# A graph layer with sorted edges on one core: spare edges of two sets at once, and single VectorE operations where there were several

## The chip, the cores and the metric

The kernel runs on one core of a Trainium2 chip. Its time is the device time of one execution in microseconds (us), and the median of several executions is what counts. Five engines work side by side, each on its own list of instructions in a fixed order: TensorE multiplies matrices, VectorE and ScalarE work element by element, GpSimd here issues the gathers (indirect DMAs), and SyncE issues the other DMAs. They wait for each other through semaphores. An engine that waits does nothing else, since it doesn't look past the instruction that waits.

## The reference

There are 12,500 nodes with 128 features each, and 400,000 edges sorted by their destination. Each edge has a type, 0 or 1.

```python
Xs = X[src]
m_data = Xs @ W_data.T + b_data
m_ctrl = Xs @ W_control.T + b_control
msg = jnp.where((edge_types == 0)[:, None], m_data, m_ctrl)
agg = jax.ops.segment_sum(msg, dst, num_segments=X.shape[0])
out = jax.nn.relu(agg + (X @ W_self.T + b_self))
x = _layernorm(x + out, axis=-1)
```

Since the sum is linear, the kernel first sums the rows `X[src]` by destination and type, and multiplies each sum with the weights afterwards. A row is kept as three bf16 parts whose sum is the f32 value.

## The kernel before

**Tiling.** 128 edges are a chunk. 125 chunks are a group, and there are 25 groups. A group alternates between windows of 5 chunks and windows of 20 chunks. For the short windows the rows of `x` are gathered from DRAM by indirect DMAs (`fetch`, L720, 865 gathers of 128 rows). For the long ones, called **sets** here, nothing is gathered: `x` lies whole in SBUF (`x3`), and rows are picked out of it by matmuls with one-hot matrices. There are 113 sets of 2,560 edges. The main loop (L1010) runs over them.

**What is done for a set.** The source of an edge is node `src & 127` of block `src >> 7`. Each of 98 blocks (100 cells with two spare ones) gets 32 places per set, and every edge has to find a place in its block's row.

1. `block_matrix` (L528) compares each edge's block with all cells: `O`, 128 x 2000. `fours` (L545) adds it up over chunks, and `same_lane` (L533) counts earlier edges of the same lane with the same block.
2. `before` (L550): TensorE multiplies the sums with a triangular matrix into the PSUM tile `rk`. `ranks` (L562) on VectorE turns this into the rank of each edge in its block: `ahead`, `prod`, three folding additions into `half`, a reduction `found` (L578) and `rank`.
3. `rank_matrix` (L602): `rm` compares the rank with 0 to 31, and two multiplications (L607) give `rv`: where the rank fits, the edge's node in one half and its code in the other (the code is its destination's offset and its type).
4. `put` (L614): 20 matmuls of `O` with `rv` write node and code of every place into `rk`. `spread` (L624) copies them out on ScalarE (`cell`), stores the nodes to DRAM (`there`) and loads them back to all 128 partitions (`pick`, 128 x 3200, 800 KB). SyncE issues both.
5. `pick_matrix` (L657): VectorE compares `pick` in place with the lane's number, in two halves. The result is the one-hot matrix.
6. `picked` (L774), one set later: 24 + 1 quads of matmuls `got` (L790) pick the rows out of `x3`, ScalarE copies them to SBUF (`emsg`, L802), VectorE makes the one-hot matrices of destinations (`esel`, L481, three for each set), and the matmuls `sums` (L676) and counts (L814) add the rows up in PSUM. `accumulate` (L707) adds that to `acc` in SBUF.

**Spare edges.** An edge whose rank is 32 or more has no place. `over` (L582) finds them: `key` keeps the packed source and code of such edges, `top` takes a lane's largest 8, and from these come their number (`over_n`) and three numbers of each (`bits`: block, node and code), copied to bf16 on ScalarE. `spare_slots` (L489) gives them up to 64 places of a further cell: the matmul `over_before` (L496, L497) counts those of lower lanes, `over_matrix` (L501) makes the one-hot matrix `om`, `turn` (L505, L507) multiplies it with `bits`, and `keep` (L512) leaves the code with the set's others and the row number in `idx` (L518). `spare_rows` (L767) gathers these rows while the set is being picked.

**Order.** In turn w of the main loop, set w is picked and added up while the places of set w + 2 are made, and the spare edges of set w + 1 get theirs. Each piece of work has a position between 0 and 1 in the turn, `merged` (L141) sorts the pieces by it, and the framework, when it builds the program, moves instructions within each engine's list again by its own estimate of when their inputs are there. So `pick`, `esel` and the work for other sets stand between the steps of `ranks`. In VectorE's list as built, the steps from `ahead` to the second `rv` stand in one run with these between them. On TensorE `put` stands within the last quads of the set that is being picked.

Beside this, each group needs once: `prep_e` (L457) and `prep_p` (L435), which prepare the codes of its edges (`erel`, L463, the destination minus the window's first one, in five operations), the pass of an overlap to the next accumulator (L700), and `finish` (L870), which multiplies the sums with the weights, normalizes and stores.

## Time and profile before

| | us |
|---|---|
| median of 3 runs (1954.3 to 1966.5) | 1956.54 |
| the profiled execution | 1946.23 |
| its span, first to last instruction | 1944.4 |
| TensorE matmuls busy | 1753.1 (90%) |
| VectorE busy | 1717.1 (88%) |
| GpSimd busy | 1362.6 (70%) |
| ScalarE busy | 1303.0 (67%) |

The granted clock of TensorE was 0.986 on average. No engine is busy all the time, and the two busiest are close to each other, so it has to be read from the waits which one holds up the other. A mean duration in the groups runs from an instruction's start to its end; the next one on VectorE starts some 0.07 to 0.09 us before that end where it needn't wait for the result (`esel` takes 0.878 us, and the next instruction starts 0.802 us after it). For sums along VectorE's list the distance from start to start is used, which the timeline shows.

The span has three stages: until about 127 us `x` is split and stored and the first sets are prepared; until about 1890 us the main loop runs; the rest ends the last group.

### The profile page before, as it was taken

The page shows a single profiled execution, that of the slowest core. Times are in us where ns is not written, and L with a number is a line of the kernel's source. Part 1 is how long each engine was busy: PE and PEld are TensorE (multiplying, and loading weights), DVE is VectorE, ACT ScalarE, POOL GpSimd, SP SyncE. Part 2 cuts the span into 40 slices and gives each one's busy share as a digit, 9 for nine tenths or more (in the row PEclk, how much of TensorE's full clock was granted, in tenths as well). Part 3 has the DMA queues.
Part 4 walks back from the last instruction along what each step waited for, and adds up shares of the span by engine and source line. Part 5 has one row for each costly group of instructions (what it writes and reads, how often), then busy time and mean ns, then how long its engine had stood idle before and what let it go on. Part 6 is the DMA issues. An engine that isn't in the chain of part 4 may idle for free.

```text
span 1944.4 us, 75191 instructions
## 1 busy us (share of the span) xinstructions
PE 1753.1 (90%) x30869; PEld 1354.9 (70%) x30869; DVE 1717.1 (88%) x4707; ACT 1303.0 (67%) x2464; POOL 1362.6 (70%) x996
## 2 busy tenths in 40 slices
PE   0669999999999999999999999999999999999996
PEld 0457777677777776777777777777777777777775
DVE  7969999999899888999999889989989889888883
ACT  4646776676676676676676667667676666766765
POOL 0378768777788777667777667787787667777760
PEclk9989999999999999999999999999999999999998
DMA  7734443443543443443444434444434344444331
GB/s 210 227 94 129 134 148 108 144 147 101 149 141 107 145 136 110 145 136 115 140 136 119 123 129 119 143 127 126 144 129 146 114 128 144 117 136 135 115 111 35
DMA packets 186533, 254.91 MB, mean 131 GB/s; under 512 B 85369, under 2 KB 152995, under 8 KB 183108
## 3 DMA queue, kind: packets, MB, share of 16 engines
q1 hardware_dynamic: 128418, 152.97, 24.6%
q0 software_dynamic: 45136, 90.65, 16.5%
q10 hardware_dynamic: 12626, 6.40, 1.2%
q8 instruction: 243, 3.98, 0.8%
q14 instruction: 110, 0.90, 0.1%
HBM read 231.89 MB, written 18.04 MB: 129 GB/s over the span
## 4 chain that ended last, share of the span: by engine, by line
DVE 53%; PE 30%; DMA 10%; issue 3%; ACT 2%; DVEq 1%; SPq 1%; POOL 0%; ACTq 0%
PE sums L676 13%; PE got L790 8%; DMA pick<-there 7%; DVE esel L481 6%; DVE pick L661 6%; DVE prod L569 5%; DVE rv L607 4%; DVE found L578 3%; DVE prod L547 3%; PE rk L619 3%; DVE half L574 3%; DVE ahead L565 3%; DVE rm L481 2%; DVE half L575 2%; DVE prod L548 2%
## 5 line engine op out<-in xcount | busy, mean ns | idle before, releaser
L725 POOL DMA_INDIRECT msg<-rows,pidx x865 | 1212.8, 1402 | 376.8 <-PE got L790 163.0
L802 ACT CAST emsg<-got 128x768 bf16<-128x768 f32 x1356 | 1026.9, 803 | 356.5 <-PE got L790 337.0
L676 PE MATMUL sums<-esel,emsg 128*128 128x176 bf16 x8136 | 748.2, 241 | 0.0
L676 PEld LDWEIGHTS <-emsg 128*128 128x128 bf16 x8136 | 596.2, 98 | 156.0 <-issue 143.2
L790 PE MATMUL got<-x,pick 128*32 128x384 bf16 x10896 | 611.6, 331 | 12.6 <-ACT emsg L802 10.1
L790 PEld LDWEIGHTS <-pick 128*32 128x32 bf16 x11074 | 250.0, 96 | 125.3 <-issue 20.3
L481 DVE TENSOR_TENSOR esel<-code_col,code 128x1408 bf16<-128x1408 bf16 x339 | 309.0, 912 | 8.8 <-PE sums L676 3.2
L769 POOL DMA_INDIRECT last<-rows,idx x113 | 145.7, 1289 | 171.7 <-DMA bias<-b_parts 70.9
L676 PE MATMUL sums<-psel,msg 128*128 128x48 bf16 x2595 | 184.9, 185 | 7.3 <-DVE acc L714 5.1
L714 DVE TENSOR_TENSOR acc<-acc,sums 128x352 f32 (+2 forms) x238 | 101.4, 426 | 96.9 <-PE sums L676 81.6
L619 PE MATMUL rk<-rv,O 128*128 128x64 bf16 x2260 | 89.6, 195 | 103.3 <-DVE rv L607 103.0
L619 PEld LDWEIGHTS <-O 128*128 128x128 bf16 x2260 | 86.1, 100 | 127.8 <-issue 126.6
L814 PE MATMUL sums<-esel,one_col 128*32 128x176 bf16 x2825 | 169.5, 242 | 2.1 <-DVE esel L481 1.2
L676 PEld LDWEIGHTS <-msg 128*128 128x128 bf16 x2595 | 149.2, 97 | 15.9 <-issue 13.3
L661 DVE TENSOR_SCALAR pick<-pick,lane_f 128x1600 bf16<-128x1600 bf16 x226 | 144.1, 643 | 17.0 <-DMA pick<-there 16.5
L761 PE MATMUL sums<-psel,one_col 128*128 128x48 bf16 x865 | 145.3, 183 | 0.0
L481 DVE TENSOR_TENSOR O<-cell_col,blk 128x2000 bf16<-128x2000 bf16 x113 | 134.2, 1188 | 4.9 <-issue 2.5
L569 DVE TENSOR_TENSOR prod<-O,ahead 128x2000 bf16<-128x2000 bf16 x113 | 134.1, 1187 | 0.0
L814 PEld LDWEIGHTS <-one_col 128*32 128x32 bf16 x2825 | 80.9, 96 | 34.0 <-issue 2.2
L565 DVE TENSOR_REDUCE ahead<-rk 128x100 bf16<-128x500 f32 x113 | 76.0, 673 | 12.0 <-PE rk L497 9.0
L627 ACT CAST cell<-rk 128x64 bf16<-128x64 f32 x113 | 23.9, 212 | 87.9 <-PE rk L619 79.1
L761 PEld LDWEIGHTS <-one_col 128*128 128x128 bf16 x865 | 82.8, 96 | 0.0
(173 smaller groups left out, 2077.0 us busy)
## 6 DMA issues: line engine op xcount, KB each, us to landing
pick<-there SPq DMA_DIRECT2D x113, 800.0 KB
acc<-acc_start SPq DMA_DIRECT2D x23, 1280.0 KB
msg<-rows,pidx POOLq DMA_INDIRECT x865
rows<-x SPq DMA_DIRECT2D x6, 1344.0 KB
xs<-in_x_dram SPq DMA_DIRECT2D x99, 62.5 KB
out_dram<-h SPq DMA_DIRECT2D x99, 62.5 KB
xt<-in_x_dram ACTq DMA_DIRECT2D x6, 896.0 KB
there<-cell SPq DMA_DIRECT2D x113, 6.2 KB
```

The costliest lines, as they stand in the source:

```text
L481: nc.vector.tensor_tensor(sel.rearrange("p n (w t) -> p n w t", t=2), col[:rows].rearrange("p (o w t) -> p o w t", o=1, t=2).to_broadcast( ...
L565: nc.vector.tensor_reduce(ahead, s["rk"][:, :CQ * NCELL].rearrange("p (c j) -> p j c", j=NCELL), AX.X, OP.add)
L569: nc.vector.tensor_tensor(prod, s["O"], ahead.rearrange("p (o j) -> p o j", o=1).to_broadcast([P, EC, NCELL]), op=OP.mult)
L619: nc.tensor.matmul(s["rk"][:m, :2 * CAP], s["held"][:, c * NCELL:c * NCELL + m], s["rv"][:, c].rearrange("p v r -> p (v r)"), start=(c == ...
L661: nc.vector.tensor_scalar(t, t, lane_f, None, op0=OP.is_equal)
L676: nc.tensor.matmul(out, msg[:, j * D:(j + 1) * D], sel, start=(start and j == 0), stop=stop, skip_group_check=True)
L725: return nc.gpsimd.indirect_dma_start(out=msg, out_offset=None, in_=rows3[:, :], in_offset=bass.IndirectOffsetOnAxis(ap=codes["p", g][0][: ...
L761: nc.tensor.matmul(cnt, one_col, sel, start=False, stop=(c == n - 1), skip_group_check=True)
L769: return nc.gpsimd.indirect_dma_start(out=msg[:OVF, :], out_offset=None, in_=rows3[:, :], in_offset=bass.IndirectOffsetOnAxis(ap=slots[w][ ...
L790: last = nc.tensor.matmul(ps[CAP * a:CAP * (a + 1), :], slots[w]["pick"][:, a * NQ + q, :], x3[:, 4 * q + a - a0].rearrange("p j d -> p (j ...
L802: nc.scalar.copy(msg, ps[:, :, :3 * D])
L814: nc.tensor.matmul(cells_of(s["ps"], EW, 1)[CAP * (q % 4):CAP * (q % 4 + 1), :], one_col[:, :CAP], s["sel"][q], start=(q < 4), stop=(q + 4 ...
```

## The change

- `prep_e`: `erel` in one `tensor_tensor` over 100 columns, with the windows' first nodes broadcast, instead of five `tensor_scalar` over 20.
- The codes and nodes of the edges, each value twice, lie interleaved in one tile `vals2` (two ScalarE copies as before, to other places), so that `rank_matrix` makes `rv` in one multiplication over 1280 columns, with `rm` read twice.
- `ranks`: one more addition folds 26 columns to 13, and `found` reduces 13 per edge instead of 26.
- `over`: `key` and `top` stay for each set, but of an even set nothing else is done; of the odd set after it, the rest is done for both sets at once, over 16 columns instead of 8. It moves from position 0.75 to 0.32.
- `over_before` moves from 0.1 (behind `before`) to 0.5, `over_matrix` from 0.28 to 0.61.
- `keep`: `idx` is made by a ScalarE activation (scale 128, bias from the tile) and no more by VectorE.
- `pick_matrix`: one comparison over 3200 columns instead of two over 1600.

```diff
-        for i in range(NE):
-            cs = slice(i * EC, (i + 1) * EC)
-            nc.vector.tensor_scalar(rel[:, cs], d[:, cs], node0[:, g, i:i + 1], None, op0=OP.subtract)
+        shape = [P, NE, EC]
+        nc.vector.tensor_tensor(
+            rel.rearrange("p (i c) -> p i c", c=EC), d.rearrange("p (i c) -> p i c", c=EC),
+            node0[:, g].rearrange("p (i o) -> p i o", o=1).to_broadcast(shape), op=OP.subtract,
+        )
...
-        codes["e", g] = (blk, twice("blk2", parts[:, 0, :]), twice("node2", parts[:, 1, :]), twice("code2", code), pk)
+        vals2 = pre.tile([P, n, 2, 2], BF, name="vals2", bufs=3)
+        for v, val in enumerate((parts[:, 1, :], code)):
+            nc.scalar.copy(vals2[:, :, v, :], val.rearrange("p (n o) -> p n o", o=1).to_broadcast([P, n, 2]))
+        codes["e", g] = (blk, twice("blk2", parts[:, 0, :]), vals2, pk)
...
-            nc.vector.scalar_tensor_tensor(idx, part[:, 0:1], 128.0, part[:, 1:2], op0=OP.mult, op1=OP.add)
+            nc.scalar.activation(idx, part[:, 0:1], AF.Identity, bias=part[:, 1:2], scale=128.0)
...
-            spares = s["spares"] = spare_slots(w - 1, rk)
-            spares[0]()
+            s["spares"] = spare_slots(w - 1, rk)
...
-            nc.vector.tensor_reduce(found, half[:, :, :26], AX.X, OP.add)
+            nc.vector.tensor_add(half[:, :, :13], half[:, :, :13], half[:, :, 13:26])
+            nc.vector.tensor_reduce(found, half[:, :, :13], AX.X, OP.add)
...
         def over():
+            ws = [w] if w % 2 == 0 else [w - 1, w]
+            if w % 2 == 0 and w < pairs - 1:
+                return
+            m = len(ws)
...
+            for k, v in enumerate(ws):
+                r = s if v == w else slots[v]
+                nc.vector.scalar_tensor_tensor(
+                    key[:, k], r["rank"][:, :, 0], CAP - 0.5, r["pk"], op0=OP.is_ge, op1=OP.mult
+                )
+                nc.vector.max(top[:, k], key[:, k])
+            full = two.tile([P, 2, 8], FP, name="full", bufs=1)
+            nc.vector.tensor_scalar(full[:, :m], top[:, :m], 0.0, None, op0=OP.is_gt)
...
+                nc.vector.tensor_reduce(over_n[:, ws[0]:w + 1], full[:, :m], AX.X, OP.add)
...
-            shape = [P, EC, CAP // 2, 2]
-            for v, val in enumerate((node2, code2)):
-                nc.vector.tensor_tensor(
-                    rv[:, :, v, :].rearrange("p c (r t) -> p c r t", t=2),
-                    rm.rearrange("p c (r t) -> p c r t", t=2),
-                    val.rearrange("p c (o t) -> p c o t", o=1).to_broadcast(shape),
-                    op=OP.mult,
-                )
+            shape = [P, EC, 2, CAP // 2, 2]
+            nc.vector.tensor_tensor(
+                rv.rearrange("p c v (r t) -> p c v r t", t=2),
+                rm.rearrange("p c (o r t) -> p c o r t", o=1, t=2).to_broadcast(shape),
+                vals2.rearrange("p c v (o t) -> p c v o t", o=1).to_broadcast(shape),
+                op=OP.mult,
+            )
...
-            (0.1, before), (0.26, ranks), (0.28, lambda: s["spares"][1]()), (0.3, rank_matrix), (0.75, over),
+            (0.1, before), (0.26, ranks), (0.3, rank_matrix), (0.32, over),
+            (0.5, lambda: s["spares"][0]()), (0.61, lambda: s["spares"][1]()),
...
-        h = NCELL // 2
-        return [(0.6 + a / 1000, lambda a=a: half(a, a + h)) for a in range(0, NCELL, h)]
+        return [(0.6, lambda: half(0, NCELL))]
```

More of the change, by code (lines that the diff above doesn't have):

```diff
@@ L183, in short_path @@
     gap = PB + EC
+    pairs = len(each_e)
     def load(g, kind):
@@ L524, in give_slots @@
         g, i = each_e[w]
-        blk, blk2, node2, code2, pk = (t[:, i * EC:(i + 1) * EC] for t in codes["e", g])
-        s = {}
+        blk, blk2, vals2, pk = (t[:, i * EC:(i + 1) * EC] for t in codes["e", g])
+        s = {"pk": pk}
         def block_matrix():
```

30 lines of the change are left out of this document (13 added, 17 removed).

## The prediction

> **What bounds the kernel now.** I read the busy time first, then who waits for whom, then the stretch of one set.
>
> ```profile
> PE 1753.1 (90%) x30869; PEld 1354.9 (70%) x30869; DVE 1717.1 (88%) x4707; ACT 1303.0 (67%) x2464; POOL 1362.6 (70%) x996
> ...
> DVE 53%; PE 30%; DMA 10%; issue 3%; ACT 2%; DVEq 1%; SPq 1%; POOL 0%; ACTq 0%
> ```
>
> TensorE and VectorE have nearly the same work, and the chain that ended last runs through both. So neither alone sets the time; the places where one waits for the other do. In the view of waits:
>
> ```profile
> PE rk L619 <- DVE rv L607: 103.0, 83, 19.0
> ...
> DVE acc L714 <- PE sums L676: 81.6, 62, 13.5
> ...
> DVE pick L661 <- DMA pick<-there: 16.5, 22, 2.2
> ```
>
> TensorE's one large wait is `put` for `rv`. Added up set by set, its idle time ahead of `put` is 72 us in the main loop (127 to 1890 us); all its idle time there is 98 us (VectorE: 177 us). The rest of the 103 us is start-up. So TensorE can give back at most 98 us in the loop, and an edit pays only as far as it lets `put` start earlier or gives TensorE other work first. The timeline of an ordinary set, one of some 15.1 us without `finish`:
>
> ```profile
> 904.40 0.52 DVE L714 TENSOR_TENSOR acc<-acc,sums 128x352 f32 x1 [0.46 <-PE sums L676]
> 905.19 0.15 DVE L518 SCALAR_TENSOR_TENSOR idx<-part 64x1 int32<-64x1 f32 x1 [0.27 <-ACT part L516]
> 905.27 0.88 DVE L481 TENSOR_TENSOR esel<-code_col,code 128x1408 bf16<-128x1408 bf16 x1
> 906.16 0.68 DVE L565 TENSOR_REDUCE ahead<-rk 128x100 bf16<-128x500 f32 x1
> 906.76 0.33 DVE L503 TENSOR_SCALAR om<-slot_col,rk 128x448 bf16<-128x448 bf16 x1
> 907.01 1.20 DVE L569 TENSOR_TENSOR prod<-O,ahead 128x2000 bf16<-128x2000 bf16 x1
> ...
> 914.03 0.47 DVE L607 TENSOR_TENSOR rv<-rm,node 128x640 bf16<-128x640 bf16 x1
> 914.43 0.47 DVE L607 TENSOR_TENSOR rv<-rm,code 128x640 bf16<-128x640 bf16 x1
> ...
> 914.95 0.76 PE L619 MATMUL rk<-rv,O 128*128 128x64 bf16 x20 [0.83 <-DVE rv L607]
> ```
>
> This is a loop through two engines: the last `sums` frees `acc`; TensorE does the next `before`; VectorE goes from `ahead` (906.16) to the end of `rv` (914.91) without a gap, 8.75 us; TensorE waits 0.83 us for it. Only what stands between `ahead` and `rv` shortens that wait. `idx` and `esel` stand ahead of it, and `ahead` would have to wait for TensorE's `before` anyway, whose matmuls end at 906.12. Sets with `finish` take 17 to 18 us and have no wait at `put`; VectorE comes out of them late, and the set behind shows 1 to 3 us of TensorE idle.
>
> **The change part by part** (VectorE, from start to start, from the timeline's rows):
>
> - `om` takes 0.25. In the order of the built program it leaves the run between `ahead` and `rv` in all 54 odd sets of places and in 24 of 54 even ones; in the other 30 it moves to just ahead of `rm` or `rv`.
> - `pick`: two of 0.55, of which both stand in the run. `om` (448 columns, 0.248) and `pick` (1600, 0.546) give 0.26 ns a column, so one of 3200 takes 0.546 + 1600 x 0.00026 = 0.96: 0.14 less. In 8 sets it leaves the run.
> - `rv`: two of 0.402. `rm` (640, 0.402) and `prod` (2000, 1.110) give 0.52 ns a column, so 1280 take 0.735: 0.07 less. Bounds: 0.735, and 1.41 at one column a cycle (the reduction `found`, 520 columns in 0.604, against `over_n`, 8 in 0.072, gives 1.04 ns a column). I take 0.735, since `esel` and the old `rv` read the same two kinds of operands, a row repeated and a pair repeated, at 0.52.
> - `found`: 260 columns at 1.04 ns take 0.33 instead of 0.60, and the extra addition 0.20 (from `half`'s row of 400 columns, 0.277, less 140 x 0.52 ns). Together 0.06 less. Its second input begins at the 14th column, an odd place that no row of before has; at 1.04 ns it would take 0.35 and the edit would lose 0.08. I take 0.20; between the two lie 0.14 us a set, 15 us in 113 sets.
> - `over`: six operations of 0.07 to 0.075 are done once for two sets: 0.22 a set less, outside the run in even sets. `idx`: 0.08 and the wait of 0.27 ahead of it go, but behind them `ahead` waits for `before`, as said; what is won is `over_before`'s 0.1 on TensorE, which no longer stands between `before` and `ahead`.
> - `erel`: five of 0.14 become one of 0.18 (as `worst`, 100 columns from two tensors): 0.5 once a group, in stretches where VectorE waits for `acc` later. Nothing, except behind `finish`.
> - ScalarE: `idx` costs between 0.16 (`part`, L516) and 0.30 (`sd`, L939); 113 times 0.3 is 34 us on an engine that is idle for 641 us, and the gather that needs it is due a quarter of a set later. The two copies into `vals2` are of the size of those removed. Nothing.
>
> VectorE has some 0.7 us a set less to do (0.14 + 0.07 + 0.06 + 0.22 + 0.08 + 0.5 x 25/113), 78 us in all. What of that becomes time is decided at `put`.
>
> *Even sets* (say w = 54). The run is `ahead` 0.60, `prod` 1.11, `half` 0.60, `pick` 0.96, `half` 0.32, `prod` 0.59, `half` 0.28, `prod` 0.33, the new addition 0.20, `eq` 0.28, `found` 0.33, `eq` 0.28, `rank` 0.09, `esel` 0.90, `rm` 0.40, `om` 0.25, `rv` 0.81 to its end: 8.3 against 8.6 by the same sum for before (8.75 in the trace). TensorE comes to `put` 7.9 us behind `before` (7.9 in the trace), or later, since in 16 of these sets counts were moved ahead of it. The wait falls from 0.83 to about 0.4: 42 ordinary sets give 18 us.
>
> *Odd sets.* Here TensorE gets a new wait: `over_before` now needs the `over_n` of the set whose rank was just found. In VectorE's list that comes behind `rv`, `top`, mostly an `esel` of 0.80, `full` and `top_i`, 9.3 us behind `before` (w = 53). TensorE's list has it ahead of `put`, but both behind nine counts, the last two `got` and most of an `add`, so it comes there after 8.6 to 10 us; `put` itself then never waits. Summed in this way over the odd sets the wait at `over_before` is 0 to 1, on average 0.4 instead of 0.83 at `put`: 43 ordinary sets give 17 us. What queues behind `over_before` is all of TensorE, `put` first.
>
> *Sets behind `finish`* (about 23): VectorE is some 1 us less late, of 1 to 3; I take 5 us in all.
>
> Against this, `put` stands 1.5 to 3 us later in the odd sets, and with it `cell`, `there` and `pick`. In the trace's DMA packets `pick` has landed 6.7 us behind the end of `put` in the median, 5.7 to 9.5 in eight tenths of the sets; the slow ones are beside `finish`. VectorE came to it after 7.6 in ordinary sets. By the new orders it comes after 6.5 to 7.5 in most and after 9 or more where `pick` was moved back; behind ten `finish` sets it now stands ahead of `prod`. I take 7 us for the waits this makes.
>
> Sum: 18 + 17 + 5 - 7 = 33 us. The profiled execution took 1946.2; that gives 1913. The median of the runs lies 10.3 us above it; with the same distance the forecast is 1923.5.
>
> [...] No row shows an operand that starts at an odd bf16 place. [...]
>
> **The rivals.**
>
> 1. *Nothing is won, since the wait only changes its place* (1956, 1940 to 1970). The odd sets' wait at `over_before` equals the old 0.83, which takes only 0.4 us of lateness of VectorE; even sets give 18 and the `pick` waits and the addition at half rate take that back. For it: VectorE's idle of 177 us shows that it is late by waiting, not by work. Against it: in every odd set TensorE now has 1 to 3 us of work between the old place of `put` and the new one.
> 2. *Slower, by late `pick`* (about 1990). Place: VectorE's `pick` ahead of or behind `prod`, with the whole run and `put` behind it. It decides once `pick` lands later than 7.3 us behind `put`. If all transfers took the 9.5 us of the slow tenth, the 54 odd sets' places would be waited for by some 2 us; less the 0.8 us that TensorE's order absorbs that is 65 us, less the 33. For it: the wait exists now (16.5 us, 22 times). Against it: the median of 6.7.
> 3. *Slower, by `rv` at one column a cycle* (about 1980): 0.67 more in each run, 0.6 of it felt in some 95 sets, is 57 us less the 33. The old `rv` speaks against it.
> 4. *More is won* (about 1885): TensorE never waits in the loop but beside `finish`, 70 us.
>
> **How the numbers follow.** A measurement here tells some 1% from no change, 20 us. Forecast (1905 to 1940): 0.55, of which 0.03 lie above 1937. More won: 0.08. Rival 1: 0.25. Rival 2: 0.08. Rival 3: 0.04. So faster by over 1% has 0.60, the same 0.28, slower 0.12. The range must leave out no more than 0.2: from 1893, which cuts half of rival 4, to 1966, which cuts rivals 2 and 3 and a little of rival 1.
>
> **What would show it.** `rv` one row of about 0.81 us, `pick` of about 1.05, `erel` of about 0.25; VectorE busy near 1640 us; TensorE's wait for `rv` down from 103 to some 45 us, and a new one of some 20 us for `over_n`; ordinary sets of 14.6 instead of 15.1 us. The prediction is wrong if `pick` is waited for in ordinary sets, if `over_before` takes over the whole wait, or if TensorE's own work between waits isn't the 14.2 us a set that the rows give.

## The result, and the profile after

The changed kernel takes 1963.78 us (median of 20 runs, 1952.3 to 1969.3), the kernel before 1949.09 (20 runs, 1941.2 to 1966.5). The ratio is 1.0064, with a 95% interval of 1.0045 to 1.0082: **0.6% slower**, where 33 us faster was forecast. (The prediction had 1956.54 for the kernel before, from three runs; over 20 runs it is 1949.09, so that 33 us less would be 1916.) In two of the five comparisons below every kernel, the one before too, took 8% longer (before: 2101.6, and 2114.5 on a chip that took 1939.0 for it in the last comparison, so that this is no kind of chip, as some expectations have it); their ratios are told, but no verdict rests on them.

The profiled execution took 1966.61, its span is 1964.7. The page of the changed kernel, busy time and chain:

```profile
PE 1769.8 (90%) x30869; PEld 1356.0 (69%) x30869; DVE 1653.0 (84%) x4045; ACT 1318.2 (67%) x2521; POOL 1187.8 (60%) x996
...
PE 41%; DVE 38%; DMA 11%; issue 4%; ACT 2%; DVEq 1%; POOL 1%; SPq 0%; ACTq 0%; POOLq 0%
PE sums L692 17%; PE got L806 11%; DMA pick<-there 8%; DVE esel L487 6%; PE rk L635 4%; DVE prod L574 3%; PE fin L934 3%; DVE pick L678 3%; DVE rv L623 3%; DVE prod L553 2%; DVE half L579 2%; DVE rm L487 2%; DVE ahead L570 2%; DVE found L584 1%; DVE half L580 1%
```

VectorE has 64 us less to do (1717.1 before; the forecast was 78) and its share of the chain fell from 53% to 38%. The time did not follow. `pick`'s transfer has 8% of the chain, some 157 us; it had 7% before. The waits after, with the total in us, how many there were and the longest:

```profile
DVE acc L730 <- PE sums L692: 104.0, 74, 5.3
...
PE rk L635 <- DVE rv L623: 37.5, 20, 19.2
PE sums L692 <- DVE acc L730: 33.2, 31, 3.2
...
DVE pick L678 <- DMA pick<-there: 28.9, 27, 2.8
PE rk L503 <- DVE over_n L605: 28.9, 35, 2.3
...
PE rk L635 <- DVE om L509: 11.6, 18, 1.1
```

TensorE's wait of 103.0 for `rv` is down to 37.5. In its place stand 28.9 for `over_n`, 11.6 for `om` and 33.2 at the sums of the short windows (L692; 5.1 before), whose PSUM buffer is free only when VectorE has done the accumulation of the window before (`acc`, L730). VectorE's wait for `pick` rose from 16.5 to 28.9.

**Where the time went.** I add up TensorE's records between the end of the ninth `put` and the end of the last one. Three terms make up that stretch: idle time; time lost to the clock (half of the time at which the granted clock stood at 0.50); and the rest, TensorE's own work.

| us | stretch | own work | idle | lost to the clock |
|---|---|---|---|---|
| before | 1697.4 | 1593.2 | 94.0 | 10.2 |
| after | 1723.4 | 1598.4 | 102.8 | 22.2 |

Then by the place of a set in its group. The first set of a group is the one whose places are made beside `finish` and the preparation of the next group; there are 23 of them in the stretch, and 81 others. A halved clock is counted for the set in which it begins.

| idle at, us | first sets, before | after | other sets, before | after |
|---|---|---|---|---|
| `put` | 24.2 | 7.9 | 44.7 | 19.8 |
| `over_before` | 0.0 | 4.8 | 0.0 | 23.9 |
| `sums` | 4.2 | 25.1 | 2.2 | 6.8 |
| `got` and others | 10.4 | 11.7 | 8.2 | 2.9 |
| all | 38.8 | 49.5 | 55.1 | 53.4 |
| lost to the clock | 5.1 | 15.4 | 5.1 | 6.8 |

The spans differ by 20.3 us: 26.0 in the stretch and 0.8 behind it are lost, 6.5 are won ahead of it. In the 81 other sets nothing was won: 25 us of waiting at `put` became 24 at `over_before`. Of the 26 us lost in the stretch, 21 (10.7 + 10.3) lie in the 23 first sets, and 5 are TensorE's own work, whose growth I can't explain.

This is one execution of each kernel. In a second profile of the changed kernel (1948.45, one of the two fastest of ten runs in a later comparison) the idle time is similar, 45.7 us in the first sets and 52.5 in the others, but the clock costs only 5.1 and 3.4. Over all runs of that comparison the mean granted clock goes from 0.9883 to 0.9863, which is worth some 4 of the 13 us between the means (an estimate: time times what is missing to 1). So the idle time repeats, and the 12 us that the clock seems to cost in the table above are in part this one execution's.

The timeline of an ordinary odd set of the changed kernel, VectorE's rows and TensorE's:

```profile
838.84 0.82 DVE L623 TENSOR_TENSOR rv<-rm,vals 128x1280 bf16<-128x1280 bf16 x1
...
839.68 0.87 DVE L487 TENSOR_TENSOR esel<-code_col,code 128x1408 bf16<-128x1408 bf16 x1
...
840.67 0.17 DVE L605 TENSOR_REDUCE over_n<-full 128x2 bf16<-128x16 f32 x1
...
840.89 0.16 PE L503 MATMUL rk<-over_n,ltri 128*128 128x1 bf16 x1 [0.98 <-DVE over_n L605]
...
841.49 0.76 PE L635 MATMUL rk<-rv,O 128*128 128x64 bf16 x20
```

`rv` was there at 839.66; TensorE stood at `over_before` from 839.91 to 840.89, since `esel` and three small operations come between `rv` and `over_n`. `put`, which needs that `rv`, has its place further back in TensorE's list and starts at 841.49. And a first set:

```profile
1175.91 0.67 DVE L570 TENSOR_REDUCE ahead<-rk 128x100 bf16<-128x500 f32 x1
1177.53 1.05 DVE L678 TENSOR_SCALAR pick<-pick,lane_f 128x3200 bf16<-128x3200 bf16 x1 [0.95 <-DMA pick<-there]
1178.50 1.20 DVE L574 TENSOR_TENSOR prod<-O,ahead 128x2000 bf16<-128x2000 bf16 x1
...
1184.60 0.31 DVE L730 TENSOR_TENSOR acc<-acc,sums 128x160 f32 x1
1184.83 0.81 DVE L623 TENSOR_TENSOR rv<-rm,vals 128x1280 bf16<-128x1280 bf16 x1
...
1184.96 0.23 PE L692 MATMUL sums<-psel,msg 128*128 128x48 bf16 x3 [1.86 <-DVE acc L730]
...
1186.39 1.95 PE L692 MATMUL sums<-esel,emsg 128*128 128x176 bf16 x12
```

`pick` stands directly behind `ahead` and waits 0.95 us for its transfer. Everything behind it in VectorE's list is late by that, the accumulation too, and TensorE stands for 1.86 us. Right behind that stall its clock halves: the twelve adds take 1.95 us, at full clock 1.08 (the next twelve, from 1189.80). The stretch of the halved clock (its bounds and length in us, then busy time and number of instructions of TensorE, its weight loads, VectorE, ScalarE and GpSimd, then the granted clock, 0.50; it is 0.93 in the 1.6 us ahead of it and 0.96 in the 2.5 us behind):

```profile
1186.50:1189.50 3.00, 3.00 (x33) 2.33 (x31) 1.86 (x6) 0.38 (x3) 2.67 (x2) 0.50 0.26 80
```

### The profile page after: what moved, and what is told of

Its sections match the earlier page's. It is cut to its first block, busy times and chain, and to the rows that moved or that the text cites. A ratio compares the mean times of both kernels' runs of the same rounds, so it can differ in the third digit from the quotient of the medians.

```text
span 1964.7 us, 74013 instructions
## 1 busy us (share of the span) xinstructions
PE 1769.8 (90%) x30869; PEld 1356.0 (69%) x30869; DVE 1653.0 (84%) x4045; ACT 1318.2 (67%) x2521; POOL 1187.8 (60%) x996
## 3 DMA queue, kind: packets, MB, share of 16 engines
q1 hardware_dynamic: 128418, 152.97, 24.2%
## 4 chain that ended last, share of the span: by engine, by line
PE 41%; DVE 38%; DMA 11%; issue 4%; ACT 2%; DVEq 1%; POOL 1%; SPq 0%; ACTq 0%; POOLq 0%
PE sums L692 17%; PE got L806 11%; DMA pick<-there 8%; DVE esel L487 6%; PE rk L635 4%; DVE prod L574 3%; PE fin L934 3%; DVE pick L678 3%; DVE rv L623 3%; DVE prod L553 2%; DVE half L579 2%; DVE rm L487 2%; DVE ahead L570 2%; DVE found L584 1%; DVE half L580 1%
## 5 line engine op out<-in xcount | busy, mean ns | idle before, releaser
L741 POOL DMA_INDIRECT msg<-rows,pidx x865 | 1071.4, 1239 | 563.5 <-PE got L806 294.9
L692 PE MATMUL sums<-esel,emsg 128*128 128x176 bf16 x8136 | 763.1, 242 | 0.0
L692 PEld LDWEIGHTS <-emsg 128*128 128x128 bf16 x8136 | 600.5, 99 | 175.1 <-issue 161.6
L806 PEld LDWEIGHTS <-pick 128*32 128x32 bf16 x11074 | 246.0, 96 | 151.2 <-issue 32.4
L487 DVE TENSOR_TENSOR esel<-code_col,code 128x1408 bf16<-128x1408 bf16 x339 | 309.1, 912 | 10.2 <-PE sums L692 4.9
L785 POOL DMA_INDIRECT last<-rows,idx x113 | 112.2, 993 | 180.0 <-ACT emsg L818 161.5
L692 PE MATMUL sums<-psel,msg 128*128 128x48 bf16 x2595 | 185.9, 185 | 33.6 <-DVE acc L730 33.2
L730 DVE TENSOR_TENSOR acc<-acc,sums 128x352 f32 (+2 forms) x238 | 101.8, 428 | 116.3 <-PE sums L692 104.0
L692 PEld LDWEIGHTS <-msg 128*128 128x128 bf16 x2595 | 149.8, 97 | 50.2 <-issue 47.9
L678 DVE TENSOR_SCALAR pick<-pick,lane_f 128x3200 bf16<-128x3200 bf16 x113 | 119.3, 1055 | 29.0 <-DMA pick<-there 28.9
L635 PE MATMUL rk<-rv,O 128*128 128x64 bf16 x2260 | 92.3, 198 | 49.2 <-DVE rv L623 37.5
L623 DVE TENSOR_TENSOR rv<-rm,vals 128x1280 bf16<-128x1280 bf16 x113 | 92.4, 818 | 0.1
```

What stands on the lines that cost most here:

```text
L487: nc.vector.tensor_tensor(sel.rearrange("p n (w t) -> p n w t", t=2), col[:rows].rearrange("p (o w t) -> p o w t", o=1, t=2).to_broadcast( ...
L623: nc.vector.tensor_tensor(rv.rearrange("p c v (r t) -> p c v r t", t=2), rm.rearrange("p c (o r t) -> p c o r t", o=1, t=2).to_broadcast(s ...
L635: nc.tensor.matmul(s["rk"][:m, :2 * CAP], s["held"][:, c * NCELL:c * NCELL + m], s["rv"][:, c].rearrange("p v r -> p (v r)"), start=(c == ...
L678: nc.vector.tensor_scalar(t, t, lane_f, None, op0=OP.is_equal)
L692: nc.tensor.matmul(out, msg[:, j * D:(j + 1) * D], sel, start=(start and j == 0), stop=stop, skip_group_check=True)
L741: return nc.gpsimd.indirect_dma_start(out=msg, out_offset=None, in_=rows3[:, :], in_offset=bass.IndirectOffsetOnAxis(ap=codes["p", g][0][: ...
```

## The experiments

**First, the parts by themselves.** The kernel before with the single operations alone:

```diff
-            nc.vector.tensor_reduce(found, half[:, :, :26], AX.X, OP.add)
+            nc.vector.tensor_add(half[:, :, :13], half[:, :, :13], half[:, :, 13:26])
+            nc.vector.tensor_reduce(found, half[:, :, :13], AX.X, OP.add)
...
-            nc.vector.scalar_tensor_tensor(idx, part[:, 0:1], 128.0, part[:, 1:2], op0=OP.mult, op1=OP.add)
+            nc.scalar.activation(idx, part[:, 0:1], AF.Identity, bias=part[:, 1:2], scale=128.0)
```

with `erel` and `rv` in one operation each as in the change; the spare edges and `pick` stay as before.

> The kernel before with the single operations alone: erel in one, rv in one, found folded once more, idx on ScalarE. The spare edges stay set by set at their old places, pick stays in two halves. Theory A (the shorter run does pay, and the two moves spoil it): the wait of TensorE at put for rv falls from 103 to about 85 us, no new wait appears, 10 to 20 us faster (1930 to 1940 beside 1950). Rival B (the wide operations spoil it: VectorE hands over later, since rv comes in one piece): not faster, and the wait for rv does not fall. Rival C (work taken off VectorE does not matter at all, the waits only change place): within 4 us of before, with the wait for rv down and another up by as much.

Measured: 1931.52 us, ratio 0.9906 [0.9880, 0.9931]. Faster by some 17 us, as theory A of this text has it (each text below has a theory A of its own); the wait for `rv` fell to 75.2, while the sums' wait for `acc` rose to 19.0. The single operations are not what spoils the change.

The kernel before with `pick` in one operation alone:

```diff
-        return [(0.6 + a / 1000, lambda a=a: half(a, a + h)) for a in range(0, NCELL, h)]
+        return [(0.6, lambda: half(0, NCELL))]
```

> The kernel before with the picks' comparison in one operation alone. Theory A: 0.14 us a set less on VectorE, but one operation that waits for the whole transfer and stands at one place: the wait of VectorE for pick goes from 16.5 to some 25 us; the time 0 to 8 us longer. Rival B (wide operations are the cause of the loss): 10 us or more slower. Rival C: within 4 us.

Measured: 1961.11, ratio 1.0065 [1.0045, 1.0086]: 13 us slower with 16 us less work on VectorE (1700.7). Of this kernel the waits:

```profile
PE rk L619 <- DVE rv L607: 118.5, 84, 19.0
...
DVE pick L661 <- DMA pick<-there: 23.7, 24, 2.4
```

TensorE waits longer for `rv`. From the first row of `ahead` to the end of `rv` VectorE now takes 8.92 us in the other sets, where it took 8.53. In the kernel before, 48 of 208 halves of `pick` stood behind `rv`, out of the way; of the whole ones 12 of 104 do. What `pick` itself takes in that run is the same, 0.81 and 0.82 us a set: what grew are waits within the run (0.10 us a set before, 0.34 now; only 0.04 of the growth is for `pick`'s transfer) and other work that now stands there. 13 us is more than theory A allowed (0 to 8) and within rival B's range, but the other wide operations gained. So it is not the length of the operation that costs; that it is the other order that the planner makes around it is my reading, which no run tests alone.

The kernel before with the spare edges of the change alone (found for two sets at once, moved):

```diff
-            (0.1, before), (0.26, ranks), (0.28, lambda: s["spares"][1]()), (0.3, rank_matrix), (0.75, over),
+            (0.1, before), (0.26, ranks), (0.3, rank_matrix), (0.32, over),
+            (0.5, lambda: s["spares"][0]()), (0.61, lambda: s["spares"][1]()),
```

> The kernel before with the spare edges alone: found for two sets at once, their count and matrix moved. Theory A (this is what spoils the change): a wait of TensorE for over_n of 25 to 35 us, the short windows' sums wait for the accumulation by 25 us or more (5 before), the wait for rv at put falls, and the time is 10 to 25 us longer (1960 to 1975). Rival B: the wide operations are at fault, so this alone gains 5 us or more. Rival C: within 4 us.

Measured: 1978.23, ratio 1.0164 [1.0136, 1.0193]: 30 us slower, the way that theory A has it, but beyond its 10 to 25 and more than the whole change. The waits:

```profile
DVE pick L673 <- DMA pick<-there: 31.6, 29, 2.4
...
PE sums L688 <- DVE acc L726: 30.7, 24, 3.7
PE rk L498 <- DVE over_n L599: 28.9, 32, 3.1
PE rk L630 <- DVE om L504: 23.4, 32, 1.1
```

The whole change, with `pick` left in two halves:

```diff
-        return [(0.6, lambda: half(0, NCELL))]
+        return [(0.6 + a / 1000, lambda a=a: half(a, a + h)) for a in range(0, NCELL, h)]
```

> The whole change, but the picks' comparison stays in two halves. If pick in one operation is what spoils it, this is 10 us or more faster than the kernel before (1940 or less). If the spare edges do (theory A), it stays at 0 to 12 us slower, with waits for over_n near 30 us and of the short windows' sums for acc near 30 us.

Measured: 1985.37, ratio 1.0198 [1.0168, 1.0228]. That is 37 us slower, outside both ranges of the expectation. So `pick` in one, which costs 13 us alone, gains 22 beside the new places of the spare edges. The parts don't add up; what one costs depends on what the others have moved.

**Which step of the spare edges.** Four kernels, in the first of the two longer comparisons. The whole change without its spare edges:

```diff
-            (0.5, lambda: s["spares"][0]()), (0.61, lambda: s["spares"][1]()),
+            (0.1, before), (0.26, ranks), (0.28, lambda: s["spares"][1]()), (0.3, rank_matrix), (0.75, over),
```

(and `over` for one set, `over_before` right behind `before`, as in the kernel before).

> The whole change without its spare edges: the single operations and the picks' comparison in one, the spare edges set by set at their old places. If the parts add up (single operations -18 us, pick in one +13), it takes 1944 beside 1949. If pick in one costs only by where the planner puts other work around it, no sum is to be had: then the wait for rv at put tells the time, near 53 us in the loop as with the single operations alone, and the time is near 1932; or near 83 as with pick alone, and it is near 1960.

Measured: ratio 0.9805 [0.9767, 0.9842], 2059.16.

The single operations with the run cleared: the third `esel`, `om` and `key` are kept behind `rv` in VectorE's list.

```diff
             if t == 3:
-                choose(16, 9)
+                made = slots.get(w + 2, {}).get("rv_ins")
+                with tc.issue_after(made.ins) if made else ExitStack():
+                    choose(16, 9)
...
-            ... (0.28, lambda: s["spares"][1]()), (0.3, rank_matrix), (0.75, over),
+            ... (0.3, rank_matrix), (0.31, behind_rv(lambda: s["spares"][1]())), (0.75, behind_rv(over)),
```

> The single operations alone (which took 1931.5), and nothing but the steps themselves, pick and the small eq left in VectorE's run from ahead to rv: the third esel (0.9 us), om (0.25) and key (0.09) are kept behind rv in its list; no work is added or removed. Theory A (the run ahead of put is what TensorE waits for, so its length is what counts): the wait at put, 53 us in the loop, falls under 15, a few us come back as waits of the sums for esel or acc, and the time is 25 to 40 us shorter than 1931 (1892 to 1906). Rival C (a wait that is removed comes back elsewhere, for VectorE has its work to do all the same): within 8 us of 1931, with the 40 us showing up as waits for esel, acc or om.

Measured: ratio 0.9757 [0.9720, 0.9794], 2052.42.

The whole change with `over_before` directly behind `put`:

```diff
-        s["tiled"] = {4: [put, spread], 6: [turn_codes, keep_codes]}
+        s["tiled"] = {4: [put, spread, lambda: s["spares"][0]()], 5: [lambda: s["spares"][1]()], 6: [turn_codes, keep_codes]}
```

> The whole change with one thing moved: over_before, the matmul that waits for the over_n of the same turn, stands behind put in TensorE's list instead of ahead of it, and om behind that. Theory A: the 29 us for over_n go, put waits some 8 us more for rv in odd sets, and the time is 15 to 25 us shorter than that of the whole change (1964): 1940 to 1950. Rival (the wait was only where VectorE's lateness came to light): the wait at put rises by the 29 us, and the time stays at 1958 to 1968.

Measured: ratio 1.0049 [1.0023, 1.0074], 2106.75. The wait for `over_n` went, and TensorE waited 44.2 us for ScalarE's `cell` in its place (both use the tile `rk`).

The whole change with the spare edges set by set, at the new places:

```diff
-            ws = [w] if w % 2 == 0 else [w - 1, w]
-            if w % 2 == 0 and w < pairs - 1:
-                return
-            m = len(ws)
...
+            key = two.tile([P, EC], FP, name="key")
+            nc.vector.scalar_tensor_tensor(key, s["rank"][:, :, 0], CAP - 0.5, s["pk"], op0=OP.is_ge, op1=OP.mult)
```

> The whole change, with its places, but the spare edges set by set, so that over_before needs the over_n of the turn before and waits for nothing. VectorE has 0.22 us a set more to do than in the whole change. Theory A (taking two sets at once is at fault, since it makes TensorE wait for work of the same turn and gives VectorE a long odd turn): no wait for over_n, fewer than 8 dips of the clock, the sums' wait for acc under 22 us, and the time is 1930 to 1945. Rival (the moved places are at fault): 1955 or more with the wait at put up instead. Rival C: within 4 us of the whole change.

Measured: ratio 0.9851 [0.9806, 0.9896], 2066.03.

In these traces TensorE stands at `got` for 80 to 103 us in the stretch (10.9 in the kernel before), since ScalarE starts its copy `emsg` some 0.3 us behind the recorded end of `got` in the median, where it is 0.105 otherwise. ScalarE itself isn't slower: it starts 0.08 us behind the event of the semaphore it waits for in both cases, but that event comes some 0.25 us and more behind `got`'s recorded end instead of 0.03. That hides what VectorE does late, so I ran them again; `over_before` this time further back, behind the adds that follow `put`:

```diff
-        s["tiled"] = {4: [put, spread], 6: [turn_codes, keep_codes]}
+        s["tiled"] = {4: [put, spread], 5: [lambda: s["spares"][0]()], 6: [lambda: s["spares"][1](), turn_codes, keep_codes]}
...
             for u in tiled.get(t, []):
-                u()
+                with tc.issue_after(final[-1].ins) if t == 5 else ExitStack():
+                    u()
```

> The kernel with the cleared run again (single operations; the third esel, om and key behind rv), since its first comparison was made on a chip on which every kernel took 8% longer and TensorE also stalled within got (0.4 to 0.7 us at a time, no releaser seen). There it was 2.4% faster than before, with a wait at put of 19 us. On a chip like that of the first comparison (before: 1949) theory A gives 1892 to 1906, rival C 1923 to 1939. From the slow chip I now lean to the upper end of A, 1905.

> The whole change without its spare edges, again, for the same reason (2.0% faster than before on the slow chip). On a chip like that of the first comparison: 1944 if the parts add up, near 1930 if pick in one costs only by where the planner puts other work around it.

> The whole change with over_before behind the last matmul of the adds that follow put in TensorE's list (directly behind put it only took on a new wait, 44 us for ScalarE's copy cell, since both use the tile rk), and om behind that. Theory A: no wait of 29 us for over_n and none for cell, some 8 us more for rv at put; the sums' wait for acc stays near 32: 1940 to 1952. Rival (the lateness only shows at the next wait): the time stays at 1958 to 1970, with put waiting for rv by 50 us or more in the loop.

> The whole change with the spare edges set by set at the new places, again, for the same reason (1.5% faster than before on the slow chip). On a chip like that of the first comparison, theory A (pairing is at fault): no wait for over_n, fewer than 8 dips of the clock, 1925 to 1940. Rival (the moved places are at fault): 1955 or more.

Measured (before: 2114.53): the ratios 0.9786 [0.9735, 0.9837], 0.9824 [0.9779, 0.9868], 0.9925 [0.9903, 0.9947] and 0.9839 [0.9785, 0.9893]. The three kernels that are the same as above repeat their ratios within the intervals; `over_before` further back is better than directly behind `put`, and still waits 27.9 us for `cell`. What follows is little: where TensorE is held up at `got`, three of the four kernels gained 1.5 to 2.4%, the cleared run most.

**Four kernels side by side, undisturbed.**

> The whole change, beside the next three on one chip. Two kinds of chips have been seen: before takes 1949 on one and 2101 to 2114 on the other, where ScalarE starts its copies of got 0.3 to 0.4 us (median) behind their input instead of 0.1. On the first kind: 1.0064 of before, as measured (1961). On the second the changed kernel was not yet measured; if pairing costs there what it cost in the first comparison, it is 0.995 to 1.01 of before, some 2% behind the kernel with unpaired spare edges (0.984, 0.985).

> The single operations alone. First kind of chip: 0.9906 of before, as measured (1931). Second kind: 0.98 to 0.985, like the kernels that have them and pick in one.

> The single operations with the third esel, om and key kept behind rv. Theory A (the run ahead of put is the bound): first kind of chip 1892 to 1906, 25 to 40 us less than the single operations alone. Rival C (a wait removed comes back elsewhere): within 8 us of the single operations alone. On the second kind, where it took 0.976 and 0.979 of before, the difference to the single operations tells the same: 15 us or more for A, under 8 for C.

> The whole change with the spare edges set by set at the new places. Theory A (pairing is at fault): 15 to 35 us less than the whole change on either kind of chip, without a wait for over_n. Rival (the moved places or the single pick are at fault): within 8 us of the whole change.

Measured (before: 1947.37): the whole change 1962.50, 1.0066 [1.0032, 1.0099]; the single operations 1932.70, 0.9936 [0.9904, 0.9968]; the cleared run 1969.74, 1.0114 [1.0056, 1.0172]; unpaired 1954.74, 1.0033 [1.0007, 1.0060].

Two theories are not borne out. *Pairing is at fault*: it costs some 8 us by the medians, and the intervals of the two overlap; it was to be 15 or more. And *the length of the run ahead of `put` is what counts* (theory A of the cleared run): from `ahead` to the end of `rv` that run is shorter by 0.57 us in the other sets (8.22; 8.79 with the single operations), and the kernel is 37 us slower than with them, where 25 to 40 faster or (rival C) within 8 was expected. Its waits:

```profile
PE rk L631 <- DVE om L509: 64.5, 72, 3.3
...
DVE pick L673 <- DMA pick<-there: 41.1, 34, 3.8
...
PE sums L688 <- DVE acc L726: 32.9, 22, 4.0
```

This is no clean test, for two things came with the edit. In TensorE's list `put` now waits for `om`, which reads `rk` and stands last; in the other sets it waits as long as before (41.7; 43.2 with the single operations). And `pick` is waited for by 41 us. Counted in VectorE's rows, the operations on `pick` that stand between `ahead` and `prod` in the 23 first sets, and what they wait for the transfer there:

| kernel | `om` | `pick` ahead of `prod` in first sets | us waited there | wait for `pick`, all | ratio |
|---|---|---|---|---|---|
| single operations (first comparison) | old place | 0 | 0 | 19.7 | 0.9906 |
| before | old place | 0 | 0 | 16.5 | 1 |
| unpaired | moved | 5 | 4.2 | 26.4 | 1.0033 |
| after | moved | 10 | 13.7 | 28.9 | 1.0064 |
| `pick` in one alone | old place | 0 | 0 | 23.7 | 1.0065 |
| cleared run | moved | 15 (halves) | 24.0 | 41.1 | 1.0114 |
| spare edges alone | moved | 16 (halves) | 19.5 | 31.6 | 1.0164 |
| change, `pick` in halves | moved | 14 (halves) | 18.4 | 38.9 | 1.0198 |

In every kernel that leaves `om` at its old place, `om` and nothing else stands between `ahead` and `prod`, in all 104 sets. Where `om` has gone, the planner puts `pick`, something else or nothing there, and `pick` above all in the first sets, where VectorE waits for it longest. There the transfer lands 9.4 us behind `put` in the median in the kernel before and 9.6 in the changed one, and `ahead`, behind which `pick` then stands, starts after 7.2 and 7.6; in the other sets the transfer lands after some 6.5 and 6.3. That it is done to fill the gap in which `prod` has to wait for `ahead`'s result is my reading; that it stands there is in the rows. The order in the table is nearly that of the waits for `pick`. `pick` in one alone does not fit: it loses as much as the whole change, with nothing but `om` there. So a new theory D: it is the place of `pick`.

**Moving `pick` alone.** It is kept behind `rv`, in the changed kernel and in the one with the single operations; no work is added or removed.

```diff
-            nc.vector.tensor_scalar(t, t, lane_f, None, op0=OP.is_equal)
+            made = slots.get(w + 1, {}).get("rv_ins")
+            with tc.issue_after(made.ins) if made else ExitStack():
+                nc.vector.tensor_scalar(t, t, lane_f, None, op0=OP.is_equal)
```

> The whole change, but the picks' comparison is kept behind rv in VectorE's list, so that nothing of the run ahead of put waits for its transfer. By now theory A has fallen (a shorter run alone did not pay); theory D: what the spare edges, the single pick and the cleared run have in common is that pick came to stand earlier in VectorE's list, ahead of prod, where in the sets beside finish it waits for its transfer (28.9 us in all for the whole change, 16.5 before) with the run, put and the accumulation behind it, and the long stalls of TensorE halve its clock. Theory D expects VectorE's wait for pick under 8 us, the idle time and lost clock of TensorE in the first set of each group (65 us over 23 sets; 44 before) under 40, and 1920 to 1942 where the whole change takes 1962 (0.985 to 0.997 of before). Rival C (the wait only moves again, now to got, which needs pick 3 us after put): within 8 us of 1962, with got waiting for pick by 20 us or more. On the slower kind of chip: 0.97 to 0.985 of before for D.

> The single operations alone, with pick (in two halves) kept behind rv. Theory D: the wait for pick (19.7 us) goes under 5, the run ahead of put is 1.1 us shorter and put's wait of 54 us in the loop falls under 20, so 1895 to 1918 where the single operations take 1932 (0.973 to 0.985 of before). Rival C: within 8 us of 1932, with got waiting for pick. On the slower kind of chip: 0.955 to 0.975 of before for D.

Measured (before: 1939.03): the changed kernel 1906.66, ratio 0.9834 [0.9790, 0.9879]; the single operations **1887.31, ratio 0.9740 [0.9694, 0.9786]**, the fastest of all. The first is faster than theory D has it (0.985 to 0.997), the second near the fast end of its range (0.973 to 0.985). The first sets of the first have 32 us of idle time and lost clock, under the 40 of theory D. The waits of the first:

```profile
PE rk L635 <- DVE rv L623: 41.4, 34, 19.2
PE rk L503 <- DVE over_n L605: 28.5, 38, 1.9
...
PE got L808 <- DVE pick L680: 15.9, 5, 14.6
PE sums L694 <- DVE acc L732: 11.0, 22, 1.7
...
DVE pick L680 <- DMA pick<-there: 0.8, 1, 0.8
```

VectorE's wait for `pick` is gone, 28.9 to 0.8, and it did not move to `got` (14.6 of the 15.9 are one wait at start-up). The sums' wait for `acc` went with it (33.2 to 11.0). The wait for `over_n`, which I had blamed, is unchanged. TensorE's wait at `put` with the single operations, which was to fall from 54 us under 20, is still 38 in the stretch. In the chain the transfer is no longer among the lines with 2% or more, and DMA has 2%, after 11%:

```profile
PE 48%; DVE 42%; issue 4%; ACT 2%; DMA 2%; DVEq 1%; SPq 0%; ACTq 0%
PE sums L694 19%; PE got L808 14%; DVE esel L487 5%; DVE prod L574 4%; PE rk L635 4%; DVE rv L623 3%; PE fin L936 3%; DVE half L579 3%; DVE ahead L570 3%; DVE prod L553 3%; DVE pick L680 2%; DVE rm L487 2%; PE rk L561 2%; DVE half L580 2%; PE rk L513 2%
```

The page of the fastest kernel, TensorE at 92%:

```profile
PE 1735.3 (92%) x30869; PEld 1340.8 (71%) x30869; DVE 1680.8 (89%) x4494; ACT 1324.4 (70%) x2577; POOL 1232.3 (65%) x996
```

The stretch of the main loop in all kernels of the undisturbed comparisons, by the same sum as above:

| us | stretch | own work | idle | lost to the clock |
|---|---|---|---|---|
| single operations, `pick` behind `rv` | 1650.3 | 1586.8 | 63.5 | 0.0 |
| change, `pick` behind `rv` | 1671.9 | 1594.7 | 72.0 | 5.1 |
| single operations, second profile | 1686.3 | 1593.0 | 86.4 | 6.8 |
| before | 1697.4 | 1593.2 | 94.0 | 10.2 |
| after, second profile | 1707.3 | 1600.6 | 98.2 | 8.5 |
| `pick` in one alone | 1713.6 | 1591.3 | 112.0 | 10.2 |
| unpaired | 1716.3 | 1589.5 | 108.1 | 18.8 |
| after, first profile | 1723.4 | 1598.4 | 102.8 | 22.2 |
| cleared run | 1724.7 | 1591.2 | 106.1 | 27.3 |
| change, `pick` in halves | 1738.0 | 1601.3 | 116.2 | 20.5 |
| spare edges alone | 1741.8 | 1593.6 | 117.5 | 30.7 |

TensorE's own work is the same within 15 us everywhere. The 91 us between the first row and the last are idle time (54), the clock that follows it (31) and 7 of own work. Moving `pick` both removes its wait and shortens the run (from 8.92 to 8.04 us in the other sets of the changed kernel, from 8.79 to 8.10 with the single operations); the two were not tried apart, so that a shorter run may pay after all when nothing else comes with it. In the first sets of the changed kernel the move takes 49.5 us of idle time to 28.8 and 15.4 lost to the clock to 3.4, in the others 53.4 to 43.3 and 6.8 to 1.7; so more than half of it (33 of 48 us; 19 of 30 by the second profile) lies where the wait was.

**What this does not show.** By the ratios the move gains some 45 us in the changed kernel (1.0066 to 0.9834), but some 38 with the single operations too (0.9936 to 0.9740), where no `pick` stood ahead of `prod`: there 9 us of the idle time go in the first sets and 14 in the others. So most of the gain is not owed to the new place that the change gave to `pick`. Beside the single operations the rest of the change (spare edges and `pick` in one) costs 30 us with `pick` where the planner puts it, and still 19 with `pick` behind `rv`. By this difference the new place is worth some 10 us. In the first sets it is nearly all of what the rest of the change costs in idle time: 36.1 us with the single operations against 45.7 to 49.5 with the change, and 27.4 against 28.8 once `pick` is moved.

Left open: why the signal behind `got` comes late in the two longer comparisons, and what the other 19 us are (pairing, the places of the spare edges with their wait of 28.5 us for `over_n`, and `pick`'s one piece are in them together). The kernel before with nothing but `pick` behind `rv`, `over_before` moved in an undisturbed comparison, and `put` free of `om` while `om` stands late were not tried.

## Why the prediction was wrong

*The sizes of the single operations held.* In the groups of the changed kernel (busy time, mean ns of one, idle time before them):

```profile
L678 DVE TENSOR_SCALAR pick<-pick,lane_f 128x3200 bf16<-128x3200 bf16 x113 | 119.3, 1055 | 29.0 <-DMA pick<-there 28.9
L623 DVE TENSOR_TENSOR rv<-rm,vals 128x1280 bf16<-128x1280 bf16 x113 | 92.4, 818 | 0.1
...
L583 DVE TENSOR_TENSOR half<-half 128x260 bf16<-128x260 bf16 x113 | 37.6, 333 | 0.0
...
L524 ACT ACTIVATE idx<-part 64x1 int32<-64x1 f32 x113 | 33.6, 297 | 3.0
L463 DVE TENSOR_TENSOR erel<-edst,node 128x100 f32<-128x100 int32 x25 | 6.3, 254 | 0.3
```

`pick` at 1.055 us (about 1.05), `rv` at 0.818 (0.81), `erel` 0.254 (0.25), `idx` 34 us on ScalarE (34), VectorE's busy time 1653 (near 1640: 64 us less of the 78). Rival 3, `rv` at 1.04 ns a column (1.41 us), is out; that this is one column a cycle, as the prediction calls it, no run shows. The new addition with its odd start takes 0.225 us from start to start in the median of the 113 sets and 0.28 at most (0.20 forecast, 0.35 at 1.04 ns a column): near the 0.20, in spite of the odd place.

*The first step that failed: the run of the ordinary sets, "8.3 against 8.6".* It did not become shorter. Summed from start to start in the 81 other sets, VectorE's work from `ahead` to `rv` is 8.35 us (even) and 8.34 (odd) before, 8.46 and 8.73 after. Term by term in the odd sets: `om` −0.27 (forecast −0.25), `rv` −0.06 (−0.07), `found` with the addition −0.03 (−0.06). But `pick` is +0.16 where −0.14 was forecast: two halves were taken as always in the run, and they were there in 60 of 82 cases; the whole one is there in all 41. `esel` is +0.20: the third one stood in the run in 35 of 41 sets, now in all, and in four sets another came in. `key` came in with 0.11, `ahead` costs 0.08 more, since `prod` behind it has to wait for its result where `om` did not (`prod` starts 0.71 us behind the start of `ahead` in the median where it follows directly, `om` started 0.60 behind it in the kernel before); parts of the accumulation, of `finish` and of the next group's preparation make up the rest. The built order has all of this; I had summed one even set of it, and followed only `om` through the others.

*"Even sets ... 18 us", "odd sets ... 17 us".* Measured in the other sets: the wait at `put` in even sets went from 21.2 to 19.3, that in odd sets from 23.4 to 0.5, with 23.9 at `over_before`. The new wait was rather well sized, 28.9 in all (about 20), and so was what is left at `put`, 49 with `om` (about 45). But the sum of the two was the old wait. That is rival 1, "the wait only changes its place", and its range (1940 to 1970) holds the result. By size this is the greater miss: 35 us were forecast here, and 2 less idle time were measured.

*"Sets behind `finish` ... 5 us"*, the step that turned the sign. They lost 21 us in the profile: 10.7 of idle time (6.9 in the second profile), 10.3 to the clock (none in the second). I had them gain by VectorE's being less late and had put 7 us for late `pick` beside it, noting that "behind ten `finish` sets it now stands ahead of `prod`". Ten it is. I priced only the wait of VectorE itself (12.4 us more in all), not what stands behind it in the list: the accumulation that frees a PSUM buffer (the sums' wait, 5.1 to 33.2, was in no term), and the halved clock behind a stall. Rival 2 had the right place for these sets. It took the odd sets as those that would wait and the median of 6.7 us against itself; over all sets the transfer lands no later (6.81 us behind `put` in the median, 6.66 before), but in the first sets it passed rival 2's mark of 7.3 in both kernels (9.4 and 9.6). It lands no later there either; it is asked for earlier.

*"Minus 7"* was thus too small, but replacing it alone doesn't mend the sum, since the 35 us of the ordinary sets were not there either. With `pick` kept behind `rv` the changed kernel is 32.4 us faster than the one before, beside the forecast 33. That the numbers meet is luck: the run is then shorter by all of `pick`, and the same move gains some 38 us without the spare edges.

*The chance of 0.60 for faster* came from TensorE having 98 us to give back (VectorE's idle time beside it is 163 us by its busy time in that window, not 177). The fastest kernel (1887) gave back a third of it: its stretch has 63.5 us of idle time beside 94.0, and is 47 us shorter with the clock and the own work. What I did not ask is what the planner would put in the place of each thing that the change took out of the run.

## What to carry to other kernels

When a scheduler orders an engine's list, taking an operation out of a critical run opens a place, and something else may come to stand there; look in the built order for what depends on a DMA. An operation that waits for a transfer belongs behind the work that another engine is waiting for: this gained some 38 and 45 us in two kernels, though VectorE's waits for the transfer summed up to only 16 and 29 us. When an experiment is to show that a place is at fault, make the same move in a kernel without the fault, as the gain there tells how much of it is something else. Sum a change over the sets with their kinds apart (here the first set of each group), with all of the built order, before believing a mean set.

## What the runs showed of the hardware

*TensorE's clock was halved at 18 of 44 stalls of 1.6 to 2 us.* In the undisturbed profiles (twelve, from 190 us on) 895 idle gaps of 0.4 to 1.6 us had a halving that began in them or within 1.5 us behind them 13 times, 128 gaps of 1.6 us and more had one 66 times, of these 44 gaps of 1.6 to 2 us 18 times. In the main loop each lasts 3.41 us or twice that, at a granted clock of 0.50, and costs half of it: in the profile of the kernel before six of 3.41 us, which are the 10.2 us lost there, in that of the changed one nine of 3.41 and two of 6.83, which are the 22.2. Why the other gaps of 1.6 us and more, 62 of the 128, had none was not shown.

*The scatter of the runs went with this clock in two kernels.* Over the 24 undisturbed runs of the kernel before in one comparison the mean granted clock goes from 0.993 to 0.983 and the time from 1936.7 to 1957.5, with a correlation of −0.95; for the changed kernel (10 runs, 0.991 to 0.981, 1948.4 to 1972.3) it is −0.93, for the single operations (10 runs, 0.994 to 0.989, 1924.7 to 1939.1) only −0.60. The fastest kernel, with no halving in its loop in the profile, stays within 6 us (1884.3 to 1890.2), but these are four runs only, and the four of the cleared run, with 27 us lost to the clock, stay within 4 (1966.9 to 1970.4). So that fewer halvings make a kernel steadier is not shown.
